# Attention over 32 images: where broadcasts, loads, statistics, one fold and one final step stand in a hand-written order of visits

## Chip, cores and metric

The kernel runs on one core of a Trainium2 chip. The metric is the time of one execution on the device, in microseconds (us); lower is better. Engines are called by the profile's names: PE is TensorE (PEld its weight loads), DVE is VectorE, ACT is ScalarE, POOL is GpSimd, SP is SyncE. In this kernel SP only issues DMAs, and POOL issues some too.

## What is computed

x has 32 images of 256 channels and 32 x 32 pixels. Each image is normalised in 32 groups of 8 channels, goes through causal attention with 8 heads of 32 channels over its 1024 pixels, and the result is added to x. All numbers are float32. Cut to what matters:

```python
def reference(x, q_w, q_b, kv_w, kv_b):
    n = group_norm(x, 32).reshape(B, C, S)            # (g - mean) / sqrt(var + 1e-5)
    q = einsum('oc,bcs->bos', q_w, n) + q_b[None, :, None]
    kv = einsum('oc,bcs->bos', kv_w, n) + kv_b[None, :, None]
    k, v = kv[:, :256], kv[:, 256:]
    q, k, v = to_multihead(q), to_multihead(k), to_multihead(v)
    scores = einsum('bhqd,bhkd->bhqk', q, k) / sqrt(32)
    scores = where(mask == 0, -10000.0, scores)       # a pixel sees earlier pixels alone
    attn = where(mask == 0, 0.0, softmax(scores))
    out = einsum('bhqk,bhkd->bhqd', attn, v)
    return x + out.transpose(0, 1, 3, 2).reshape(B, 256, 32, 32)
```

## The kernel before

The work of one image, called a batch here, is cut into 12 visits (`N = 12`): two groups `g` of four heads, six visits each. A visit takes a set of blocks of keys and queries. Its `scores` (L339) are PE products of `k` and `q` into three PSUM tiles `sT` (L302), three exponentials on ACT into `e` and `eh` (L384, L380), and in visits 0, 1, 3 and 5 of a group a mask on POOL, which writes the tile `diagonal` (L330). One visit later `values` (L399) multiplies the exponentials by `v` on PE into `acc` (L409), and `add_keys` (L421) adds exponentials on DVE, in place (L427). So an addition that overwrites a tile waits until PE has read it.

The softmax is divided out at the end. For each batch there are four sums `n` (two groups of heads by two halves of the queries). Each is 128 partitions by 2048 numbers and is reduced in steps:

- `fold(b, n, 64)` and `fold(b, n, 32)` (L436): DMAs issued by POOL that add the upper half of the partitions to the lower, 512 KB and 256 KB by the profile. The second waits for the first.
- `stack(b, n)` (L442): an SP DMA that puts the remaining 32 partitions into `folded`. It waits for the second fold.
- `sum_folded` (L448): DVE transposes and reductions, in visits 6 and 7 of the next batch.
- `invert` (L485), in visit 8: DVE takes reciprocals, and SP writes them to DRAM (L494) and reads them back four times, broadcast over 32 partitions each, into `rb` (L499). `rb` has one buffer.
- `finish(b, n)` (L519): on DVE a product `num * rb` (L524), two additions of the bias and x (L526) and for the first half a copy of one column (L531), then an SP DMA to the output (L532).

Beside this, a later batch is prepared: four loads of x by SP (L107), two `norm_channels` on DVE (L172: two `BATCH_NORM_STATS2` and an aggregate for 128 channels), `norm_mean` on PE and ACT (`pm`), `norm_deviation` on DVE (`dev`, L195 to L197), `norm_variance` on PE and ACT (`pv`), `norm_rstd` on POOL (L217, L219), `norm_apply` on ACT. The twelve projections of a batch (`pp` and `ppv`, L162) stand one to a visit.

The order is written by hand. Before the program is emitted, each step is entered under the number of a visit with `when`, counted over all batches (batch b begins at visit 12 b). In the main loop a visit i emits its scores, then the steps in `at`, then values and additions of visit i - 1, then the steps in `after`. This order is kept for PE, ACT, DVE and POOL (`manual_schedule`). SP isn't in that list: a scheduler orders its DMAs, and the visit is not a wait. The tables are these, where the numbers in PROJECT and PREPARE count from the first visit of the batch that is prepared:

```python
PREPARE = (-14, -13, -9, -9, -8, -8, -7, -6, -5, -3)
SUMS = (3, 7, 11, 13)
FINISH = (N + 13, N + 13, N + 14, N + 15)
```

The first two of PREPARE are the two `norm_channels`, the third `norm_mean`, the fourth `norm_deviation`, the fifth `norm_variance`. Sum n is folded at SUMS[n] (64 partitions) and two visits later (32), and stacked two visits after that. In visits of a batch, counted modulo 12, the statistics stand in visits 10 and 11, `dev` in 3, the final steps in 1, 1, 2 and 3.

Of the kernel before, what the change touches and what calls it, by code (L numbers as in the profile page):

```python
# [9 lines left out]
F32 = mybir.dt.float32  # L10
# [7 lines left out]
P = 128  # L18
HD = 32
CPG = 8  # L20
HALF = 512
# [11 lines left out]
def tile_norm_attention_residual(  # L33
# [19 lines left out]
    nc = tc.nc  # L53
# [4 lines left out]
    NH = S // HALF  # L58
# [22 lines left out]
        out=avg, in_=avg, pattern=[[-CPG, P // CPG], [0, CPG]],  # L81
# [3 lines left out]
        out=avg, in_=avg, pattern=[[CPG, P // CPG], [0, CPG]],  # L85
# [13 lines left out]
    def unshifted():  # L99
        live = {}  # L100
# [3 lines left out]
        def load_part(b, g, cols):  # L104
            if (g, cols.start) == (0, 0):
                live["x", b] = xpool.tile([P, NG, S], F32, tag="x", name=f"x_{b}")
            nc.sync.dma_start(out=live["x", b][:, g, cols], in_=x_in[b, :, g, cols])  # L107
# [6 lines left out]
        work = tc.alloc_tile_pool(name="work", bufs=2)  # L114
# [3 lines left out]
        dram = tc.alloc_tile_pool(name="dram", bufs=2, space=bass.MemoryType.DRAM)  # L118
# [9 lines left out]
        def load_weights():  # L128
            for n, w in enumerate((q_w, kv_w[0:C], kv_w[C : 2 * C])):
                live["wn", n] = epool.tile([P, 4, HALFBANK], F32, tag="eh", bufs=3, name=f"wn_{n}")[:, :NG, :C]  # L130
                nc.sync.dma_start(out=live["wn", n], in_=w.rearrange("(o p) c -> p o c", p=P))
            nc.sync.dma_start(out=qk_bias[:, 0, :], in_=q_b.rearrange("(g p) -> p g", p=P))
            nc.sync.dma_start(out=qk_bias[:, 1, :], in_=kv_b[0:C].rearrange("(g p) -> p g", p=P))
            nc.sync.dma_start(out=v_bias_col, in_=kv_b[C : 2 * C].rearrange("(g p) -> p g", p=P))
# [346 lines left out]
        def check(rows, least, most):  # L481
            nc.vector.scalar_tensor_tensor(in_range, rows, least, in_range, ALU.is_ge, ALU.mult)
            nc.vector.scalar_tensor_tensor(in_range, rows, most, in_range, ALU.is_le, ALU.mult)

        def invert(b):  # L485
            rows = live["rows", b]
            check(rows, SUM_MIN, SUM_MAX)
            inv = small.tile([P, ROW], F32, tag="inv", name=f"inv_{b}")
            nc.vector.reciprocal(inv, rows)
            turned = small.tile([P, ROW], F32, tag="inv_turned", name=f"inv_turned_{b}")  # L490
            nc.vector.transpose(turned, inv)

            spread = dram.tile([2, 4, 2, HALF], F32, tag="inv", name=f"inverses_{b}")
            nc.sync.dma_start(  # L494
                out=spread.rearrange("a n j (m c) -> (n j m) a c", c=HD), in_=turned.rearrange("p (a c) -> p a c", a=2),
            )
            live["rb", b] = work.tile([P, 4, HALF], F32, tag="rb", bufs=1, name=f"rb_{b}")
            for h in range(4):
                nc.sync.dma_start(  # L499
                    out=live["rb", b][h * HD : (h + 1) * HD],  # L500
                    in_=spread[h // 2, :, h % 2, :].unsqueeze(0).broadcast_to([HD, 4, HALF]),
                )

        def invert_here(b, n, within=slice(0, HALF)):

# [57 lines left out]
        N, TOTAL = NG * len(VISITS), 2  # L563
# [42 lines left out]
        def when(i, f, where=at):  # L606
            where.setdefault(i, []).append(f)
# [11 lines left out]


        PROJECT = (-5, -4, -3, -2, -1, 0, 1, 2, 3, 4, 5, 6)
        PREPARE = (-14, -13, -9, -9, -8, -8, -7, -6, -5, -3)
        SUMS = (3, 7, 11, 13)
        FINISH = (N + 13, N + 13, N + 14, N + 15)
        every = range(4)

        with tc.manual_schedule(engines={ENG.PE, ENG.Activation, ENG.DVE, ENG.Pool}):


            load_weights()  # L630
            if B > 1:
                load(1)
            junk = small.tile([P, 1], F32, tag="most", name="junk")
            nc.scalar.activation(junk, ones, AF.Exp)
            keep_busy(16)
            for g in range(NG):
                norm_channels(0, g)
            norm_mean(0)

            live["less_mean"] = work.tile([P, 4, HALF], F32, tag="folded", bufs=1, name="less_mean")[:, 0, :]  # L640
            for s in range(2):
                nc.scalar.activation(
                    blocks(live["less_mean"], s), blocks(live["x", 0][:, 1, :HALF], s, s == 1), AF.Identity,
                    bias=live["minus_mean", 0][:, 1:2],
                )
            turn_weights(0)
            norm_deviation(0)
            norm_variance(0)
            norm_rstd(0)
            for hf in range(NH):  # L650
                for g in range(NG):
                    norm_apply(0, hf, g)
                if hf == 0:
                    for n in (1, 2):
                        turn_weights(n)
                    keep_busy(3)
                    nc.vector.tensor_scalar_mul(qk_bias[:, 0, :], qk_bias[:, 0, :], SCALE)  # L657
            units = projections(0)
            for n, f in zip((None, None, None, 0, 0, 0) + PROJECT[6:], units):
                if n is None:  # L660
                    f()
                else:
                    when(n, f)
            if B > 1:
                prepare(1, (None, None, 0, 1, 2, 2, 3, 4, 5, 7))
            for b in range(B):
                first, last = b * N, b == B - 1
                if b >= 1:
                    for n, f in zip(PROJECT if not last else PROJECT[:-1] + (7,), projections(b)):
                        when(first + n, f)  # L670
                if b >= 2:
                    for n in range(NG * NH):
                        cols = slice(n % NH * HALF, (n % NH + 1) * HALF)
                        when(max(first - 2 * N + 7 + n // 3, 0), lambda b=b, n=n, cols=cols: load_part(b, n // NH, cols))
                    prepare(b, [first + n for n in PREPARE])
                if not last:
                    for n in every:
                        v = first + SUMS[n]
                        when(v, lambda b=b, n=n: fold(b, n, 2 * HD), after)
                        when(v + 2, lambda b=b, n=n: fold(b, n, HD), after)  # L680
                        when(v + 4, lambda b=b, n=n: stack(b, n))
                    late = b == B - 2
                    v = first + N + (5 if late else 6)
                    when(v, lambda b=b: sum_folded(b, every[:2]), after)
                    when(v + 1, lambda b=b: sum_folded(b, every[2:]), after)
                    when(v + 2, lambda b=b: invert(b))
                    for n in every:
                        v = first + (N + 9 + n // 2 if late else FINISH[n])
                        when(v, lambda b=b, n=n: finish(b, n), after)
                else:  # L690
                    when(first + 3, lambda: sums(0, SUMMED[1], False), after)
                    when(first + 7, lambda: sums(1, SUMMED[5], False), after)
                    when(first + 9, lambda: sums(2, SUMMED[7], False), after)
                    when(first + 8, lambda b=b: invert_here(b, 0))
                    when(first + 9, lambda b=b: finish(b, 0))
                    when(first + 8, lambda b=b: invert_here(b, 1))
                    when(first + 8, lambda b=b: finish(b, 1))
                    when(first + 10, lambda b=b: invert_here(b, 2))
                    when(first + 11, lambda b=b: finish(b, 2), after)
            for i in range(B * N + 1):  # L700
                if i < B * N:
                    scores(*divmod(i, N))
                for f in at.pop(i, ()):
                    f()
                b, v = divmod(i - 1, N)
                if i == B * N:

                    sums(3, SUMMED[v], False)
                if i:
                    values(b, v)  # L710
                    if b < B - 1 or v not in SUMMED or v == 1:
                        add_keys(b, v)
                if i in (B * N - 2, B * N - 1):

                    sums(3, SUMMED[v])
                for f in after.pop(i, ()):
                    f()
            assert not at and not after
            outside = end_last(B - 1)
# [170 lines left out]
```

## Time and profile before

| | |
|---|---|
| median of three runs | 1830.64 us (1828.4 to 1831.34) |
| the profiled execution, its own time | 1833.26 us |
| its span, first to last instruction | 1831.6 us |
| granted TensorE clock, mean | 0.997 of full |
| one batch in the second half (start of a `pv` to that of the next) | 55.77 us |
| DMA traffic | 236.77 MB, mean 129 GB/s |
| POOL's DMA queue, share of 16 engines | 36.4% |
| SP's DMA queue, share of 16 engines | 27.5% |

The profile is of one execution. A line of waits reads "engine tile line <- releaser: total us, times, longest us"; "issue" is time in which the engine waited for nothing that the profile shows. A line of a timeline reads "start us, length us, engine, line, operation, output<-inputs, shapes, count", and in brackets the idle time ahead of it and what ended it; merged lines give the whole stretch. "SPq" and "POOL ... DMA_DIRECT2D" are DMA issues and not the transfers. In the list of DMA queues, the columns are packets, MB and the share of 16 engines' span; q0 is POOL's queue, q1 SP's, q8 and q14 carry instructions.

### The profile page before, as it was taken

The numbers are of one execution on the slowest core, as the hardware profiler recorded it, in microseconds if no ns is written. First come the engines' busy times: TensorE is split into PE (matmuls) and PEld (weight loads), VectorE is DVE, ScalarE is ACT, GpSimd is POOL, SyncE is SP. The second block draws the span as 40 slices with busy tenths as digits, with TensorE's granted clock in tenths as the row PEclk, the third lists the DMA queues.
The fourth block names the chain that finished last, engine by engine and source line by source line (L and its number), as shares of the span: only waits on it lengthen the run. The fifth ranks groups of instructions, "written<-read, shape, count | busy, mean of one in ns | idle before, by whom it ended". The sixth has DMA issues, their size and how long they took to land.

```text
span 1831.6 us, 81672 instructions
## 1 busy us (share of the span) xinstructions
PE 1801.3 (98%) x37036; PEld 961.8 (53%) x37036; DVE 1639.0 (89%) x1832; ACT 1456.0 (79%) x1985; POOL 877.6 (48%) x901
## 2 busy tenths in 40 slices
PE   9999999999999999999999999999999999999997
PEld 5555555555555555555555555555555555555553
DVE  4689999888898988999999999999999998999987
ACT  6888878877788877888877888878888778888784
POOL 2444544534445445454554454554545544545531
PEclk9999999999999999999999999999999999999999
DMA  3457676666755767667767667676676666676662
GB/s 122 66 101 147 129 146 118 122 144 129 148 113 121 152 123 147 117 125 149 142 133 132 123 139 147 136 142 119 122 151 136 137 132 121 139 147 135 123 115 82
DMA packets 86530, 236.77 MB, mean 129 GB/s; under 512 B 21280, under 2 KB 22304, under 8 KB 70304
## 3 DMA queue, kind: packets, MB, share of 16 engines
q0 software_dynamic: 15872, 97.53, 36.4%
q1 hardware_dynamic: 70304, 133.96, 27.5%
q8 instruction: 290, 4.75, 1.0%
q14 instruction: 64, 0.52, 0.1%
HBM read 66.85 MB, written 34.57 MB: 55 GB/s over the span
## 4 chain that ended last, share of the span: by engine, by line
PE 88%; DVE 9%; issue 2%; ACT 0%; DMA 0%; POOL 0%; DVEq 0%
PE sT L302 27%; PE pp L162 26%; PE acc L409 24%; PE ppv L162 10%; DVE diagonal L427 3%; DVE e L427 2%; DVE rb L526 2%; DVE num L524 1%; PE pd L461 0%; PE pv L162 0%; ACT e L384 0%; DMA x<-in_x_dram 0%; DVE dev L197 0%; DVE dev L196 0%; DVE rb L531 0%
## 5 line engine op out<-in xcount | busy, mean ns | idle before, releaser
L384 ACT ACTIVATE e<-sT 128x1024 f32<-128x1024 f32 x768 | 745.0, 1022 | 261.0 <-PE sT L302 261.0
L330 POOL TENSOR_SCALAR_AFFINE_SELECT diagonal<-eh 128x512 f32<-128x512 f32 x512 | 580.8, 1157 | 768.2 <-ACT eh L380 765.7
L302 PE MATMUL sT<-q,k 32*64 32x128 f32 (+2 forms) x18432 | 584.3, 372 | 0.4 <-issue 0.3
L427 DVE TENSOR_TENSOR e<-e,e 128x1024 f32<-128x1024 f32 x315 | 539.3, 1712 | 30.8 <-ACT v L266 13.6
L302 PEld LDWEIGHTS sT<-q,k 32*64 32x64 f32 x18432 | 405.5, 131 | 181.2 <-PE sT L302 59.5
L162 PE MATMUL pp<-xn,wT 128*32 128x512 f32 x4096 | 492.2, 598 | 0.2 <-DVE qk_bias L657 0.2
L409 PE MATMUL acc<-e,v 128*32 128x384 f32 (+3 forms) x4608 | 405.2, 451 | 2.3 <-issue 2.2
L380 ACT ACTIVATE eh<-sT 128x768 f32<-128x768 f32 (+1 forms) x384 | 341.1, 888 | 0.0
L409 PEld LDWEIGHTS acc<-e,v 128*32 128x32 f32 x4608 | 150.9, 110 | 265.1 <-issue 242.4
L162 PE MATMUL ppv<-wT,xn 128*32 128x256 f32 x4096 | 252.8, 383 | 8.4 <-issue 8.4
L162 PEld LDWEIGHTS pp<-xn,wT 128*32 128x32 f32 x4096 | 107.2, 109 | 198.9 <-issue 164.3
L427 DVE TENSOR_TENSOR diagonal<-diagonal,e 128x1536 f32<-128x1536 f32 x126 | 187.9, 1492 | 25.8 <-PE acc L409 10.6
L427 DVE TENSOR_TENSOR e<-e,eh 128x1024 f32<-128x1024 f32 x127 | 179.2, 1411 | 6.5
L409 PEld LDWEIGHTS acc<-diagonal,v 128*32 128x32 f32 x4096 | 124.6, 110 | 86.1 <-issue 73.1
L162 PEld LDWEIGHTS ppv<-wT,xn 128*32 128x32 f32 x4096 | 120.8, 109 | 92.0 <-issue 20.6
L409 PE MATMUL acc<-diagonal,v 128*32 128x128 f32 x4096 | 162.0, 273 | 0.0
L427 DVE TENSOR_TENSOR e<-e,diagonal 128x2048 f32<-128x2048 f32 x62 | 140.5, 2266 | 23.5 <-POOL diagonal L330 23.5
L440 POOL DMA_DIRECT2D e<-e x124 | 111.5, 899 | 75.5 <-issue 38.2
L526 DVE SCALAR_TENSOR_TENSOR rb<-num,v_bias_col,x 128x256 f32<-128x256 f32 x248 | 133.5, 579 | 4.4
L235 ACT ACTIVATE xn<-x,shift,rstd 128x256 f32<-128x256 f32 x248 | 137.1, 613 | 0.0
L427 DVE TENSOR_TENSOR e<-e 128x512 f32<-128x512 f32 x64 | 62.6, 978 | 72.6 <-PE acc L409 72.6
L440 POOL DMA_DIRECT2D diagonal<-diagonal x124 | 111.6, 900 | 0.2 <-issue 0.2
(78 smaller groups left out, 1075.2 us busy)
## 6 DMA issues: line engine op xcount, KB each, us to landing
diagonal<-diagonal POOLq DMA_DIRECT2D x62, 512.0 KB, 6.5
e<-e POOLq DMA_DIRECT2D x62, 512.0 KB, 7.3
rb<-inverses SPq DMA_DIRECT2D x124, 256.0 KB, 4.7
out_dram<-rb SPq DMA_DIRECT2D x124, 256.0 KB, 7.6
x<-in_x_dram SPq DMA_DIRECT2D x120, 256.0 KB, 6.1
diagonal<-diagonal POOLq DMA_DIRECT2D x62, 256.0 KB, 4.6
folded<-diagonal SPq DMA_DIRECT2D x62, 256.0 KB, 6.0
e<-e POOLq DMA_DIRECT2D x62, 256.0 KB, 5.2
```

Source lines behind the costliest of these rows:

```text
L162: nc.tensor.matmul(out[part], lhsT=lhsT[:, part], rhs=rhs, start=start, stop=stop, skip_group_check=True)
L235: nc.scalar.activation(to, of, AF.Identity, bias=live["shift", b][:, g : g + 1], scale=rstd)
L302: return nc.tensor.matmul(bank[c : c + KEYS, cols], lhsT=live["k", b, g][rows, kb * P + c : kb * P + c + KEYS], rhs=live["q", b, g][rows, ...
L330: nc.gpsimd.affine_select(out=square[:, :, place + s * P : place + (s + 1) * P], in_=raw[:, :, (1 - s) * KEYS : (3 - s) * KEYS], pattern=[ ...
L380: exp = nc.scalar.activation(eh.rearrange("p (n bank) q -> p bank n q", n=2)[:, :, :, :narrow], short[:, :, :, :narrow], AF.Exp)
L384: nc.scalar.activation(e[:, 2 * a : 2 * a + 2, :wide], pairs[a][:, :, :wide], AF.Exp)
L409: nc.tensor.matmul(acc[HD * j : HD * (j + 1), of], lhsT=live["v", b][:, kb, h * HD : (h + 1) * HD], rhs=e[:, j, :], start=first, stop=last ...
L427: nc.vector.tensor_add(to, to, tile_of(b, g, at))
L440: nc.gpsimd.dma_start(out=total[:rows], in_=total[rows : 2 * rows], accum_op=ALU.add)
L524: nc.vector.tensor_mul(num, num, rb)
L526: nc.vector.scalar_tensor_tensor(blocks(rb, s), blocks(num, s, s == 1), v_bias_col[:, g : g + 1], blocks(xt[:, g, cols], s), ALU.add, ALU.add,
```

## The change

Nothing is computed differently, and the number of instructions of each kind that work on data is the same. Five things move:

- The write of the inverses stays in `invert`; the four broadcasts become `spread_inverses(b, h)` and are entered under visits 8, 9, 10 and 11 (for the batch before the last all under the same visit as `invert`).
- The four loads of x are entered under visits 7, 8, 11 and 12, where it was 7, 7, 7 and 8.
- The two `norm_channels` are entered two visits later, at -12 and -11.
- The folds and the stack of the third sum are entered one visit earlier, at 10, 12 and 14.
- The last of the four final steps is entered one visit later, at N + 16.

```diff
-            spread = dram.tile([2, 4, 2, HALF], F32, tag="inv", name=f"inverses_{b}")
+            spread = live["spread", b] = dram.tile([2, 4, 2, HALF], F32, tag="inv", name=f"inverses_{b}")
             nc.sync.dma_start(
                 out=spread.rearrange("a n j (m c) -> (n j m) a c", c=HD), in_=turned.rearrange("p (a c) -> p a c", a=2),
             )
-            live["rb", b] = work.tile([P, 4, HALF], F32, tag="rb", bufs=1, name=f"rb_{b}")
-            for h in range(4):
-                nc.sync.dma_start(
-                    out=live["rb", b][h * HD : (h + 1) * HD],
-                    in_=spread[h // 2, :, h % 2, :].unsqueeze(0).broadcast_to([HD, 4, HALF]),
-                )
+
+        def spread_inverses(b, h):
+            if h == 0:
+                live["rb", b] = work.tile([P, 4, HALF], F32, tag="rb", bufs=1, name=f"rb_{b}")
+            nc.sync.dma_start(
+                out=live["rb", b][h * HD : (h + 1) * HD],
+                in_=live["spread", b][h // 2, :, h % 2, :].unsqueeze(0).broadcast_to([HD, 4, HALF]),
+            )
...
-        PREPARE = (-14, -13, -9, -9, -8, -8, -7, -6, -5, -3)
-        SUMS = (3, 7, 11, 13)
-        FINISH = (N + 13, N + 13, N + 14, N + 15)
+        PREPARE = (-12, -11, -9, -9, -8, -8, -7, -6, -5, -3)
+        SUMS = (3, 7, 10, 13)
+        LOADS = (7, 8, 11, 12)
+        FINISH = (N + 13, N + 13, N + 14, N + 16)
...
-                        when(max(first - 2 * N + 7 + n // 3, 0), lambda b=b, n=n, cols=cols: load_part(b, n // NH, cols))
+                        when(max(first - 2 * N + LOADS[n], 0), lambda b=b, n=n, cols=cols: load_part(b, n // NH, cols))
...
                     when(v + 2, lambda b=b: invert(b))
+                    for n in every:
+                        when(v + 2 + (0 if late else n), lambda b=b, n=n: spread_inverses(b, n))
```

## The prediction

> **What bounds the kernel now.** I read the page first, then TensorE's waits in two windows, the chain of waits over one period, and the timelines of VectorE, GpSimd's queue and SP's queue over the same period. The page says that TensorE is busy nearly all the time, so only what still makes it wait can be won:
>
> ```profile
> PE 1801.3 (98%) x37036; PEld 961.8 (53%) x37036; DVE 1639.0 (89%) x1832; ACT 1456.0 (79%) x1985; POOL 877.6 (48%) x901
> q8 instruction: 290, 4.75, 1.0%
> ```
>
> TensorE's waits from 100 to 700 us, then from 700 to 1740 us (columns: total us, times, longest):
>
> ```profile
> PE ppv L162 <- issue: 8.4, 9, 1.9
> PE acc L409 <- issue: 2.2, 2, 1.9
> ```
>
> ```profile
> PE pv L162 <- DVE dev L197: 5.9, 18, 0.3
> ```
>
> Two different losses. In the second half every batch loses 0.33 us, because `pv` (the variance product) waits for `dev`, the end of a VectorE chain. There a batch takes 55.77 us, of which TensorE is busy 55.44. In the first half that wait is absent, and TensorE stops instead with nothing that the profile names, 10.6 us in all, nearly always inside the `ppv` of visit 3.
>
> The chain of waits around one such `pv` (start, us, what) shows how the first loss arises: `dev` stands last in a VectorE queue that has no gap, behind the last of the four final steps.
>
> ```profile
> 776.74 0.61 DVE num L524
> 777.38 0.88 DVE rb L526 x2
> 778.26 0.08 DVE dev L195
> 778.56 0.17 DVE dev L197
> 778.87 0.24 PE pv L162 x5
> ```
>
> The unnamed stops are late instruction fetches. The 290 packets of the instruction queue are TensorE's: 290 x 256 instructions are its 74,000 matmuls and weight loads, so there is a fetch every 256 instructions, nine per batch. In the trace's packets a fetch normally starts when some 160 instructions of the block before it have run. Before the stop at 604.82 us it started only at 602.93, 222 instructions later than that; the GpSimd folds had kept the 16 DMA engines busy since 595.7, and it started when they ended. There are 61 such long bursts (a 256 KB and a 512 KB fold issued together, 7 us). A fetch wanted 1.8 to 2.1 us after a burst's start was served 4.1 to 6 us after it (one at 8.6); one wanted 1 to 1.7 us ahead of it, at +2.3 to +4.7 (one at 6.5); one wanted 2.15 us or more after it, mostly only at its end, 6 to 8.7 us. TensorE stops when the fetch has ended about 415 to 448 instructions into the old block. The boundary moves by two instructions a batch, which is why this ends midway.
>
> GpSimd's folds, with issue time, over one period; the pairs at 877 and 887 are the long bursts, 860.50 and 868.53 are single:
>
> ```profile
> 860.50 0.81 POOL L440 DMA_DIRECT2D e<-e  x1 [1.25 <-issue]
> 868.53 0.84 POOL L440 DMA_DIRECT2D diagonal<-diagonal  x1
> 877.18 0.80 POOL L440 DMA_DIRECT2D diagonal<-diagonal  x1
> 877.71 1.13 POOL L440 DMA_DIRECT2D e<-e  x1
> ```
>
> **What the Trainium skill says.** "Runtime: NRT & Kernel Launch", section "Instruction fetch mechanics": instructions come in 16 KiB blocks of 256 and the cost of a boundary is mostly hidden. The trace agrees on the size (4.75 MB in 290 packets), and not on the cost here, 10.6 us. "DMA: Bandwidth & Descriptors", section "Queues, rings and completion order": each DMA engine takes its queues in turn, a packet at a time. That would let a fetch through soon; the trace shows it held for 5 us, so I use the measured delays. "SBUF — State Buffer", section "SBUF: two separate sides": a VectorE operation with two SBUF inputs and a GpSimd one exclude each other. The trace agrees: the `num` product beside a mask takes 1.11 us, alone 0.68.
>
> **Part by part.**
>
> *Broadcasts and loads, one to a visit.* SP's order isn't written by hand. In the order of the built programs the four `rb` broadcasts still follow the write of the inverses back to back, and the four loads of x still stand together ahead of the stack of the first sum. An SP DMA waits for data, not for a visit: before, they went out as soon as they could,
>
> ```profile
> 837.62 4.45 SPq L107 DMA_DIRECT2D x<-in_x_dram  x4
> 856.33 1.97 SPq L499 DMA_DIRECT2D rb<-inverses  x4
> ```
>
> and will again. Cost and gain 0 (bounds: -1 to +1 us, from the 1.97 us in which they are issued). Cover if the broadcasts did spread: they land about 861.5, `finish` first reads `rb` at 876.7, 15 us of slack.
>
> *Statistics from visits 10 and 11 to 0 and 1.*
>
> ```profile
> 862.64 1.28 DVE L177 BATCH_NORM_STATS2 st<-x 128x6 f32<-128x512 f32 x2
> 863.96 0.21 DVE L178 BATCH_NORM_AGGREGATE mv<-st 128x2 f32<-128x12 f32 x1
> 875.70 1.03 DVE L427 TENSOR_TENSOR e<-e 128x512 f32<-128x512 f32 x1 [1.38 <-PE acc L409]
> 880.54 3.09 DVE L427 TENSOR_TENSOR diagonal<-diagonal,e 128x1536 f32<-128x1536 f32 x2 [0.27 <-issue]
> 889.72 0.15 DVE L195 TENSOR_TENSOR dev<-mv,mean 128x2 f32<-128x2 f32 x1
> ```
>
> Each set is 1.44 us (862.64 to 864.08). Taking both from ahead lets VectorE reach the add at 875.70 earlier, but that add waits for TensorE. The first set fits in the 1.38 us idle there plus the 2.88 us freed, less some 2 us now spent waiting for a mask: free. The second lands between the second final step and the `diagonal` adds: +1.44, of which the 0.27 us wait is swallowed: +1.17 us ahead of `dev`. Its result is needed by `pm` at 885.2 and ready at 881.7. The x that they read was loaded 30 us before.
>
> *The last final step a visit later.* Its product and two additions, 888.21 to 889.72, leave the place ahead of `dev`: -1.51 us. Together 1.17 - 1.51 = -0.34, so `dev` ends at 890.27 - 0.34 = 889.93. `pv` could start at 890.08, 0.14 us after `dev`, so 889.94 is just in time. Overlaps with the mask at 884.27 shift from the additions to a product; I take that as even, +-0.4 us. VectorE has 58 more semaphore instructions, two a batch; those in the trace run under the preceding operation. I leave 0.05 us a batch over 29 batches, 1.5 us: **5.9 - 1.5 = -4.4 us**. Bounds: -5.9, and +9 if `dev` is 0.3 later instead. Its output DMA goes out 4 us later on SP; behind it stand the loads of x, about 1 us later, needed 30 us on. In SP's order the third stack now stands ahead of the first three outputs, which wait about 3 us for its fold; `rb` is rewritten only 30 us later.
>
> *The fold of the third sum, a visit earlier.* Its two DMAs move on GpSimd's queue: the 512 KB one from 868.53 to just behind the 256 KB `e` fold at 860.50, ahead of a mask that starts at 866.32 anyway; the 256 KB one to before a mask, at about 874.9. The latter breaks up the pair at 877, and its burst (878.6 to 885.6) ends about 3 us sooner. That is the burst in which the fetches of the first half were late: 222 instructions late less 3 us x 41 a us is 100, far from a stop. It also frees the 512 KB `e` fold, for which the pair at 887 waits 1.3 us. **-9.6 of the 10.6 us** (bounds 0 and -10.6). In exchange 860.50 becomes a pair: a burst from 862.0 to about 868.5, with a fetch wanted between -1.5 and +0.8 us of its start. By these measurements it is served at about +4.5 where it was at +1.0 to +2.7: 2 us, some 80 to 90 instructions, on ends of 263 to 359. Most stay under 415; about 9 late batches may stop 0.4 us: **+3.5 us** (bounds 0 and +27).
>
> Sum: 1833.26 (the profiled execution, 1.7 us over its span) - 4.4 - 9.6 + 3.5 = 1822.8. The median of the runs is 2.6 us lower than that execution, so 1820.
>
> **Rivals.** *The spread is nothing and the fetches stay late*, because they hang on the outputs and not on the fold: only 4.4 us remain, 1826. For: outputs fill the engines right after that burst. Against: the fetches start with the fold's end. *No change*: the second statistics and a slowed product keep `dev` late and the new pair costs what the old one gives back: 1830. *Slower*: the new pair at 861 holds its fetch to the burst's end, at +6.5 instead of +4.5. A stop of 1 us in each of 27 batches is +27, against -14 gained: 1844. It decides once the fetch is served more than 5 us after it is wanted. Against it: the pairs whose fetch was wanted before +2.1, of which two in over thirty were served that late.
>
> **Chances.** Forecast 0.5 (1814 to 1827), fetches stay late 0.2 (1824 to 1829), no change 0.15 (1827 to 1834), slower 0.15 (1834 to 1850). About 0.2% (3.7 us) is what a measurement can tell from no change. Faster: 0.5 + 0.15 of the second; same 0.05 + 0.15; slower 0.15. The range 1814 to 1834 leaves the slower case out.
>
> **What would show it.** Right: no `pv` wait on `dev`; unnamed stops of TensorE under 4 us; a batch of 55.4 to 55.5 us; SP's four broadcasts still issued within 2 us; the fold pair at 860 instead of 877. Wrong: TensorE stops near the `acc` or `sT` of visits 10 and 11, or `pv` waits on. A longer batch with TensorE fully busy would refute the whole account.

## The result and the profile after

The changed kernel takes 1813.72 us (median of 4 runs, 1813.51 to 1814.04), the kernel before 1829.97 us on the same chip (4 runs, 1828.4 to 1831.34): a ratio of 0.9912, 95% interval 0.9894 to 0.9929. That is 16.25 us less (0.9%), where the prediction had 10 us less. The profiled execution took 1813.86 us, its span is 1812.2 us.

The same two lines of the page as before the change (busy us, share of the span, instructions; then packets, MB and share of the instruction queue):

```profile
PE 1797.5 (99%) x37036; PEld 956.9 (53%) x37036; DVE 1643.0 (91%) x1832; ACT 1457.2 (80%) x1985; POOL 919.4 (51%) x901
q8 instruction: 290, 4.75, 1.1%
```

TensorE's waits from 100 to 1780 us. In the same stretch of the kernel before they were 8.4 us in `ppv`, 5.9 in `pv`, 2.2 in `acc` and 0.3 in `sT`:

```profile
PE sT L302 <- issue: 0.3, 1, 0.3
PE pp L162 <- issue: 0.3, 1, 0.3
PE pv L162 <- DVE dev L197: 0.2, 1, 0.2
```

The chain of waits around one `pv`, and the windows view of one batch, from a `pv` to the next (after the window: its length, then the busy time of PE, PEld, DVE, ACT and POOL, the clock, the DMA share and GB/s):

```profile
763.00 1.29 PE acc L409 x24
764.30 0.12 PE pv L162 x8
764.41 0.90 PE sT L302 x17
```

```profile
764.17:819.61 55.44, 55.44 (x1159) 29.50 (x1153) 51.63 (x58) 45.44 (x62) 29.80 (x28) 1.00 0.68 136
```

The chain no longer leaves TensorE for VectorE. `pv` follows the last `acc` at once, and a batch takes 55.44 us instead of 55.77. Both of the losses that the prediction named are all but gone from the view of waits. TensorE looks full in the 55.44 of this last line. It isn't, as e10 and e11 show below.

GpSimd's queue shows the moved fold, and SP's queue that the spread did nothing: the 512 KB fold of `diagonal` now stands right behind that of `e` at 790.88, the one at 803.90 is single, and the four broadcasts are issued in one go.

```profile
790.88 0.81 POOL L440 DMA_DIRECT2D e<-e  x1 [1.25 <-PE pp L162]
791.43 1.11 POOL L440 DMA_DIRECT2D diagonal<-diagonal  x1
...
803.90 0.78 POOL L440 DMA_DIRECT2D diagonal<-diagonal  x1
```

```profile
787.69 1.76 SPq L501 DMA_DIRECT2D rb<-inverses  x4
```

### The profile page after: what moved, and what is told of

Same layout as the page of the kernel before. It is cut to its first block, busy times and chain, and to the rows that moved or that the text cites. A ratio compares the mean times of both kernels' runs of the same rounds, so it can differ in the third digit from the quotient of the medians.

```text
span 1812.2 us, 81732 instructions
## 1 busy us (share of the span) xinstructions
PE 1797.5 (99%) x37036; PEld 956.9 (53%) x37036; DVE 1643.0 (91%) x1832; ACT 1457.2 (80%) x1985; POOL 919.4 (51%) x901
## 4 chain that ended last, share of the span: by engine, by line
PE 98%; DVE 1%; ACT 0%; issue 0%; DMA 0%; POOL 0%; DVEq 0%
PE sT L302 30%; PE acc L409 27%; PE pp L162 26%; PE ppv L162 13%; PE pd L461 0%; ACT e L384 0%; PE pv L162 0%; DMA x<-in_x_dram 0%; DVE diagonal L427 0%; DVE st L177 0%; DVE e L427 0%; PE pm L162 0%; POOL diagonal L330 0%; ACT eh L380 0%; DVE rb_last L528 0%
## 5 line engine op out<-in xcount | busy, mean ns | idle before, releaser
L330 POOL TENSOR_SCALAR_AFFINE_SELECT diagonal<-eh 128x512 f32<-128x512 f32 x512 | 649.1, 1291 | 748.6 <-ACT eh L380 748.4
L427 DVE TENSOR_TENSOR e<-e,e 128x1024 f32<-128x1024 f32 x315 | 553.6, 1757 | 21.6 <-ACT v L266 4.8
L162 PE MATMUL ppv<-wT,xn 128*32 128x256 f32 x4096 | 247.5, 382 | 0.0
L409 PEld LDWEIGHTS acc<-diagonal,v 128*32 128x32 f32 x4096 | 119.6, 110 | 92.9 <-issue 75.7
L440 POOL DMA_DIRECT2D e<-e x124 | 102.3, 825 | 38.1 <-PE pp L162 31.1
L528 DVE SCALAR_TENSOR_TENSOR rb<-num,v_bias_col,x 128x256 f32<-128x256 f32 x248 | 117.5, 514 | 4.4
L440 POOL DMA_DIRECT2D diagonal<-diagonal x124 | 119.4, 963 | 0.0
L526 DVE TENSOR_TENSOR num<-num,rb 128x512 f32<-128x512 f32 x124 | 110.8, 894 | 0.0
```

What stands on the lines that cost most here:

```text
L162: nc.tensor.matmul(out[part], lhsT=lhsT[:, part], rhs=rhs, start=start, stop=stop, skip_group_check=True)
L330: nc.gpsimd.affine_select(out=square[:, :, place + s * P : place + (s + 1) * P], in_=raw[:, :, (1 - s) * KEYS : (3 - s) * KEYS], pattern=[ ...
L409: nc.tensor.matmul(acc[HD * j : HD * (j + 1), of], lhsT=live["v", b][:, kb, h * HD : (h + 1) * HD], rhs=e[:, j, :], start=first, stop=last ...
L427: nc.vector.tensor_add(to, to, tile_of(b, g, at))
L440: nc.gpsimd.dma_start(out=total[:rows], in_=total[rows : 2 * rows], accum_op=ALU.add)
L526: nc.vector.tensor_mul(num, num, rb)
```

## Experiments

The theory to be tested was that of the prediction: `pv` waits for `dev` until the last final step moves, and late instruction fetches stop TensorE until the pair of folds at 877 is broken up. The rivals: only one of the two pays, or the gain comes from elsewhere (the broadcasts, the loads, the statistics). Each ratio is to the kernel before on the same chip, whose medians lie between 1829.3 and 1831.4 us from one group of runs to the next.

### Each part alone, put into the kernel before

**e1, the fold alone.**

```diff
-        SUMS = (3, 7, 11, 13)
+        SUMS = (3, 7, 10, 13)
```

Expected: 

> Only the third sum's folds move a visit earlier. Two losses (my theory: late instruction fetches behind the paired folds, and pv waiting for dev): the unnamed stops of TensorE fall from 10.6 us to under 1.5, but pv now waits 0.33 us for dev in all 29 batches, 9.6 us where it was 6.3; together -7, about 1823. Rival, one VectorE chain causes both losses: 1830, as nothing moves on VectorE. Rival, the spread of broadcasts and loads does it: 1830.

Measured: 1831.6 us, ratio 1.001 (1.0002 to 1.0017). By itself the fold's move is worth nothing, slightly less. Its waits:

```profile
PE pv L162 <- DVE dev L197: 9.9, 30, 0.4
PE sT L302 <- issue: 6.5, 15, 0.6
```

The stops in `ppv` are gone as foreseen, but the new pair makes 15 others, in `sT` of visit 10. And `pv` now waits in every batch (29 times from 100 us on), where it waited in 18: a batch that had lost its time in `ppv` had given VectorE the time to finish `dev`.

**e2, the final step alone.**

```diff
-        FINISH = (N + 13, N + 13, N + 14, N + 15)
+        FINISH = (N + 13, N + 13, N + 14, N + 16)
```

Expected: 

> Only the last final step moves a visit later. My theory: dev ends 1.5 us earlier, the pv wait (5.9 us) goes, the unnamed stops in the first half stay near 10.6 us: 1824. Rival, one VectorE chain behind both: 1814. Rival, spread: 1830.

Measured: 1821.56 us, ratio 0.9958 (0.9943 to 0.9973). 8.9 us are gained, though the view of waits had shown only 5.9 on `dev` in all. No wait on `dev` is left between batches; the stops in `ppv` stay (7.8 us in 9).

**e3, the statistics alone.**

```diff
-        PREPARE = (-14, -13, -9, -9, -8, -8, -7, -6, -5, -3)
+        PREPARE = (-12, -11, -9, -9, -8, -8, -7, -6, -5, -3)
```

Expected: 

> Only the statistics move two visits later. My theory: dev ends 1.17 us later, so pv waits about 1.5 us in every batch without an unnamed stop: +1.17 x 18 and up to 1.5 x 11, 1851 to 1867, so slower than before. Rival, the statistics are hidden wherever they stand because VectorE has 3.7 us idle in a batch: 1830.

Measured: 1851.45 us, ratio 1.012 (1.0102 to 1.0138).

```profile
PE pv L162 <- DVE dev L197: 30.2, 26, 1.4
```

Most of these waits are 1.38 us where they had been 0.33: the statistics hold `dev` up by 1.05 us a batch, close to the 1.17 of the prediction. Alone this part is a loss.

**e4, broadcasts and loads alone** (the loads at 7, 8, 9 and 10, since the statistics still need x in visits 10 and 11).

```diff
+        LOADS = (7, 8, 9, 10)
...
+                    for n in every:
+                        when(v + 2 + (0 if late else n), lambda b=b, n=n: spread_inverses(b, n))
```

Expected: 

> Only the broadcasts are entered one to a visit and the loads of x at visits 7, 8, 9, 10 (the last two before the statistics, which stand at 10 and 11 here). My theory: SP's queue holds its DMAs in the same order and they go out as soon as data is there: 1830, the four broadcasts issued within 2 us. Rival, the spread frees the DMA engines for the fetches: unnamed stops under 2 us, 1820 or less.

Measured: 1829.96 us, ratio 1.0001 (0.9987 to 1.0015), and the stops are as before: 7.6 us in `ppv`, 6.0 on `dev`.

### Is it the instruction fetch?

TensorE's first work in the kernel is a loop of products that nothing uses, `keep_busy(16)`. Six more or six fewer of its rounds put 24 instructions more or fewer ahead of everything, and so shift where each block of 256 ends against the folds. Nothing else changes.

**e8, 24 instructions more.**

```diff
-            keep_busy(16)
+            keep_busy(22)
```

Expected: 

> The kernel before with six more filler products (24 instructions) on TensorE at the very start, nothing else. If the unnamed stops are late instruction fetches, each boundary of 256 instructions falls 24 instructions earlier, where it stood 12 batches later: the stops of batches 3 to 11 vanish, under 2 us stay, pv waits for dev in all batches instead: -10.6 + 3.6 + up to 2.1 us of the filler itself, 1823 to 1826. If the stops belong to the early batches for another reason (HBM, start of the run): 1830 to 1832, stops of 10 us in the first 650 us.

Measured: 1826.03 us, ratio 0.9975 (0.9968 to 0.9983).

```profile
PE pv L162 <- DVE dev L197: 9.6, 29, 0.4
```

Every stop in `ppv` is gone, without a fold moved. As in e1, `pv` then waits in all batches, so that only 4.5 us of the gain remain. By the starts of the batches, some 6 us are lost beyond these waits (each priced at 0.46 us, as in e12 below), in other places.

**e9, 24 instructions fewer.**

```diff
-            keep_busy(16)
+            keep_busy(10)
```

Expected: 

> The kernel before with six filler products fewer (24 instructions) at the very start. Late fetches: each boundary falls 24 instructions later, so the stops last 12 batches longer, up to about 1320 us instead of 650, some 18 us of stops in all: 1836 to 1840. Another reason tied to the early batches: 1830, stops as before.

Measured: 1861.01 us (1851.29 to 1869.63), ratio 1.0172 (1.0114 to 1.023), far beyond what was expected.

```profile
PE ppv L162 <- issue: 13.4, 16, 2.4
PE acc L409 <- issue: 8.4, 6, 2.4
PE sT L302 <- issue: 6.2, 4, 3.4
```

So the unnamed stops depend on where the boundaries of blocks fall, and on nothing that the 24 instructions compute. In the traces' packets the late fetches follow: of 290, those that ended 415 or more instructions into the old block are 12 in the kernel before, 6 in e8, 29 in e9 and 1 in the changed kernel. The trace shows nothing but the fetch that goes by these boundaries. The runs also show that the kernel before stood by chance in a bearable place.

### One part taken out of the changed kernel

**e5, without the fold's move.**

```diff
-        SUMS = (3, 7, 10, 13)
+        SUMS = (3, 7, 11, 13)
```

Expected: 

> The changed kernel with the third sum's folds back in visits 11, 13, 15. My theory: no pv wait, unnamed stops come back, near 10 us: 1824. Rival, one VectorE chain causes both losses: 1814, no stops.

Measured: 1826.31 us, ratio 0.9981 (0.9972 to 0.999). The stops in `ppv` are back, 6.4 us in 8. With the other parts in place the fold's move is worth 12.6 us (1826.31 to the 1813.72 of the changed kernel), alone it was worth nothing (e1).

**e6, without the final step's move.**

```diff
-        FINISH = (N + 13, N + 13, N + 14, N + 16)
+        FINISH = (N + 13, N + 13, N + 14, N + 15)
```

Expected: 

> The changed kernel with the last final step back in visit 3 (N + 15). My theory: dev ends 1.5 us later than in the changed kernel, pv waits about 1.4 us in each of 29 batches, no unnamed stops: 1814 + 41 = 1855. Rival, VectorE's idle time takes it up: 1814.

Measured: 1861.87 us, ratio 1.0178 (1.0162 to 1.0195): `pv` waits 37.6 us on `dev` in 30 waits, and 6.4 us of stops stand in `sT`. The time is 7 us over the theory's 1855, which had no such stops.

**e7, without the statistics' move.**

```diff
-        PREPARE = (-12, -11, -9, -9, -8, -8, -7, -6, -5, -3)
-        LOADS = (7, 8, 11, 12)
+        PREPARE = (-14, -13, -9, -9, -8, -8, -7, -6, -5, -3)
+        LOADS = (7, 8, 9, 10)
```

Expected: 

> The changed kernel with the statistics back at visits 10 and 11 (and so the last two loads entered at visits 9 and 10). My theory: dev ends another 1.2 us earlier than needed, nothing won and nothing lost: 1814, no pv wait, no unnamed stops. Rival, moving the statistics is part of the gain (it takes VectorE's load off visits 10 and 11): 1816 or more.

Measured: 1819.1 us (1817.78 to 1822.56), ratio 0.9945 (0.993 to 0.996). This missed: the part that loses 21 us alone gains 5.4 here.

```profile
PE sT L302 <- issue: 5.8, 15, 0.6
```

The new pair stops TensorE in `sT` as in e1, and in the changed kernel it hardly does. What differs is when the pair goes out. In the trace's DMA packets, over 28 batches (times from the batch's `pv`, those of the fetch from the start of the burst; medians):

| | `e` fold issued | burst starts | fetch wanted | served | ended over 400 instructions into the old block |
|---|---|---|---|---|---|
| e7 | 25.85 | 27.3 | +0.55 | +4.1 | 8 of 28 |
| changed kernel | 26.71 | 28.65 | -0.85 | +2.05 | 1 of 28 |

The pair is 0.86 us later in the changed kernel and the burst 1.35, and then most fetches are wanted before the burst begins. Set beside the starts of a batch of e11 (below), which has no stop there, 21 of 29 batches of e7 lose time at this place, 13.0 us in all, where the view of waits shows 5.8 us in `sT` and 1.3 in `pp`. In 12 of the 21 the fetch ended only 334 to 387 instructions into the old block, so the count of those over 400 is too low a measure. In the changed kernel 3 batches lose 1.4 us there.

The mask in front of the pair explains most of the delay, 0.73 of the 0.86 us (GpSimd's queue; first the changed kernel, its `pv` at 764.17, then e7, its `pv` at 766.8):

```profile
786.36 3.27 POOL L330 TENSOR_SCALAR_AFFINE_SELECT diagonal<-eh 128x512 f32<-128x512 f32 x2 [6.50 <-ACT eh L380]
```

```profile
788.82 2.54 POOL L330 TENSOR_SCALAR_AFFINE_SELECT diagonal<-eh 128x512 f32<-128x512 f32 x2 [6.37 <-ACT eh L380]
```

With the statistics moved, VectorE reaches its addition of `diagonal` 0.9 us later in the batch (20.3 and 19.4 us after `pv`), and that addition covers more of the mask. VectorE's lines, again the changed kernel first:

```profile
784.47 3.09 DVE L427 TENSOR_TENSOR diagonal<-diagonal,e 128x1536 f32<-128x1536 f32 x2
```

```profile
786.21 3.09 DVE L427 TENSOR_TENSOR diagonal<-diagonal,e 128x1536 f32<-128x1536 f32 x2
```

"SBUF — State Buffer", section "SBUF: two separate sides", says that a VectorE operation with two SBUF inputs and a GpSimd one that reads SBUF exclude each other; both traces agree, 3.27 against 2.54 us for the same mask. So the statistics would gain by an accident: they delay a mask, which delays a pair. That was then put to the test.

### Is it the delay of the pair?

**e10: e7, with the pair held up by something else.** Six memsets on GpSimd stand in front of it.

```diff
             if (n, rows) == (1, HD):
                 nc.gpsimd.drain()
+                for _ in range(6):
+                    nc.gpsimd.memset(inv_last, 1.0)
```

Expected: 

> The changed kernel with the statistics left in visits 10 and 11, as in e7, and six small memsets on GpSimd (about 0.14 us each, a constant tile that is rewritten with other contents, read by nothing until the end) between the mask of visit 9 and the pair of folds, so that the pair goes out about 0.85 us later, where the statistics' move had put it. Theory: the move of the statistics gains only because VectorE then holds up that mask and with it the pair, so the fetch gets ahead of the burst; with the memsets the stops in sT of visit 10 (5.8 us in 15 stops in e7) fall under 1 us, and the time goes from 1819.1 to 1814-1815.5. Rival: the statistics' own place matters (VectorE's queue ahead of a wait of TensorE), and the memsets change nothing or cost: 1818-1821, stops as in e7.

Measured: 1809.52 us (1808.15 to 1811.85), ratio 0.9888 (0.987 to 0.9905). The `e` fold goes out 26.70 us after `pv`, as in the changed kernel. The burst starts at 28.1, the fetch is wanted 0.2 us ahead of it and served at +2.7 (medians), and 2 of 28 end over 400 instructions into the old block. In `sT` two stops are left:

```profile
PE sT L302 <- issue: 1.5, 2, 1.3
```

So the delay of the pair by itself is worth some 9.6 us (1819.1 to 1809.52, on two chips on which the kernel before took 1829.26 and 1829.65), more than the whole gain of the statistics' move, 5.4. That the memsets do better than the statistics, by 4.2 us, the expectation had not foreseen. Start to start, a batch takes 55.31 us here in most cases, against 55.45 in the changed kernel. The order of TensorE's instructions is the same in both, so I compared their starts within a batch: the step of 0.14 us comes at the `acc` of a `diagonal`, 13.5 us after `pv`. The mask for it, in the changed kernel and then in e7:

```profile
772.83 4.73 POOL L330 TENSOR_SCALAR_AFFINE_SELECT diagonal<-eh 128x512 f32<-128x512 f32 x2 [1.09 <-ACT eh L380]
```

```profile
775.43 3.72 POOL L330 TENSOR_SCALAR_AFFINE_SELECT diagonal<-eh 128x512 f32<-128x512 f32 x2 [2.11 <-ACT eh L380]
```

VectorE's lateness stretches this mask too, by 1.0 us, and its last piece, a memset (L337), now ends too late. Who waits for that memset, in the changed kernel:

```profile
  PEld acc L409: 5.6, 28
```

In e7, e10 and the kernel before, nobody waits for it. In e5, where the statistics and the final step are moved too, the weight loads wait for it 18 times, and a batch mostly takes 55.43 us there. The wait stands in the view of the weight loads, not in that of the products. No run takes this wait away by itself, so its price is read from the starts, 0.14 us a batch.

**e11: no pair at all.** e7 again, but the third sum's first fold stays in visit 11, and only its second fold and its stack come a visit earlier.

```diff
-        SUMS = (3, 7, 10, 13)
+        SUMS = (3, 7, 11, 13)
...
-                        when(v + 2, lambda b=b, n=n: fold(b, n, HD), after)
-                        when(v + 4, lambda b=b, n=n: stack(b, n))
+                        when(v + (1 if n == 2 else 2), lambda b=b, n=n: fold(b, n, HD), after)
+                        when(v + (3 if n == 2 else 4), lambda b=b, n=n: stack(b, n))
```

Expected: 

> As e7 (the changed kernel with the statistics left in visits 10 and 11), but the third sum's first fold stays in visit 11, as before the change, and only its second fold and its stack come a visit earlier. So neither the pair at 860 nor the one at 877 is formed. Theory: with no long burst near a boundary that is wanted, neither ppv of visit 3 nor sT of visit 10 stops, and pv doesn't wait, since the finish is moved: 1814-1816, unnamed stops under 2 us. Rival: a fold in another place holds the fetch as well, or GpSimd's queue is held by the second fold and delays masks: 1818-1826.

Measured: 1806.02 us (1805.76 to 1807.87), ratio 0.9871 (0.9854 to 0.9888), below what either theory had said. TensorE's waits from 100 to 1780 us:

```profile
PE sT L302 <- issue: 0.5, 1, 0.5
```

Of the 29 batches 27 take 55.31 us. It beats both kernels, the changed one by 7.7 us (0.4%).

### What does the wait for `dev` cost?

e11 opened a question on the first term of the prediction: if a batch takes 55.31 us without waits, then the 55.44 that the prediction took as TensorE's work contains some.

**e12: e11 with the final step in its old place.**

```diff
-        FINISH = (N + 13, N + 13, N + 14, N + 16)
+        FINISH = (N + 13, N + 13, N + 14, N + 15)
```

Expected: 

> As e11 (no pair at 860, none at 877, statistics in visits 10 and 11), but the last final step is back in its place of before, so that pv waits for dev in every batch and nothing else stops TensorE. This measures the price of the dev wait by itself over 29 batches. Theory: the batch without any wait is 55.31 us (as in e11), and the gap that the trace shows as 0.33 us costs 0.46, since the modelled ends of the matmuls ahead of it hide 0.13: 1806.0 + 29 x 0.46 = 1819.4, batches of 55.77. Rival, the prediction's reading: the batch without the wait is 55.44 and the wait costs the 0.33 that the view of waits shows: 1806.0 + 29 x 0.33 = 1815.6, batches of 55.64.

Measured: 1819.5 us (1819.18 to 1820.3), ratio 0.994 (0.9925 to 0.9954). The theory's number, to 0.1 us. TensorE's waits from 100 to 1780 us:

```profile
PE pv L162 <- DVE dev L197: 9.7, 29, 0.3
```

TensorE's timeline at one `pv`, and the windows view of the batch after it, first e11:

```profile
816.22 0.62 PE L409 MATMUL acc<-diagonal,v 128*32 128x128 f32 x16
816.70 0.24 PE L162 MATMUL pv<-dev,avg 128*32 128x2 f32 x8
```

```profile
816.70:872.01 55.31, 55.31 (x1160) 29.55 (x1152) 52.23 (x58) 45.38 (x62) 26.01 (x28) 1.00 0.69 136
```

Then e12:

```profile
822.22 0.62 PE L409 MATMUL acc<-diagonal,v 128*32 128x128 f32 x16
823.17 0.24 PE L162 MATMUL pv<-dev,avg 128*32 128x2 f32 x8 [0.33 <-DVE dev L197]
```

```profile
823.17:878.95 55.78, 55.45 (x1153) 29.58 (x1153) 52.17 (x58) 45.37 (x62) 28.86 (x28) 1.00 0.69 135
```

Without the wait `pv` starts 0.48 us after the group of `acc`, ahead of the 0.62 at which that group ends by the profile. With it, it starts 0.95 after. The wait costs the difference of the starts, 0.47 us, and the profile shows 0.33, for it counts from the modelled end. The missing 0.14 is booked as busy time: 55.45 against 55.31 for the same work.

## Why the prediction was too high

The mechanisms of the prediction held, and every sign that it gave for being right came: no wait of `pv` on `dev` but one of 0.2 us, unnamed stops of 0.6 us, a batch of 55.44 us, the broadcasts in one go, the pair at 860. Its sizes did not hold. The runs can be chained, so that each step differs in one thing, apart from the spread of broadcasts and loads, worth nothing by e4, and the memsets of e10 (medians in us):

| from, to | what differs | predicted | measured |
|---|---|---|---|
| before to e12: 1831.4 to 1819.5 | the pair at 877 is broken up | -9.6 | -11.9 |
| e12 to e11: 1819.5 to 1806.0 | the last final step a visit later | -5.9 + 1.5 | -13.5 |
| e11 to e10: 1806.0 to 1809.5 | the new pair, at its later time | +3.5 | +3.5 |
| e10 to the changed kernel: 1809.5 to 1813.7 | the statistics, all but the delay of the pair | 0 | +4.2 |

The predicted column sums to -10.5. The measured one sums to -17.7 from the 1831.4 of that group's runs of before. The -16.25 of the result starts from 1829.97. The first and the last step are the least certain: by the interval of e12's ratio the -11.9 lies between -8 and -14, and the last step goes from one group of runs to another.

**What failed is the size of both losses**, "5.9 - 1.5 = -4.4 us" and "-9.6 of the 10.6 us". Both were read as the idle time that the view of waits shows, with "TensorE is busy 55.44" as the floor. The floor is 55.31 (e11), and counted from start to start both losses are larger:

- A wait on `dev` costs 0.46 or 0.47 us and not 0.33 (e12). With the stops still there, the 18 waits of the trace are then 8.3 us and not 5.9, and 8.9 were measured (e2).
- In the profile of the kernel before, the 11 batches without such a wait take 17.4 us more than 11 x 55.31, where the view shows stops of 10.6.

The two losses also overlap. The prediction saw that "in the first half that wait is absent" but not why: the stops in `ppv`, just ahead of `pv`, gave `dev` its time. Take the stops away (e1, e8, e12) and `pv` waits in nearly every batch, 28 or 29 of 29. So how the gain is shared out depends on the order. In the table the pair goes first: of the 17.4 us, 11 x 0.46 = 5.1 come back as waits, which leaves 12.3, and 11.9 were measured. Then the final step ends 29 waits: 29 x 0.46 is 13.3, and 13.5 were measured. With the final step first it is 8.9 (e2), then 15.5 (e2 to e11). Both together are 23.6 us (e11), where 5.9 and 9.6 had been put.

**The 1.5 us for more semaphore instructions and a close `dev`** is not seen at `pv`: only one wait of 0.2 us on `dev` is left between 100 and 1780 us.

**The statistics** do cost ahead of `dev` what the prediction said, 1.05 us against 1.17 (e3), and the final step pays for it. What it left out is that VectorE then stays late, by 1 us eight us after `pv` and by 0.9 us twenty us after it. This has two effects beyond `dev`, both through the mask on GpSimd: +4.2 us by the mask at 772.83, whose memset TensorE's weight loads await (29 x 0.14 is 4.1), and, by the measure of e10, -9.6 us by the mask at 786.36, which delays the new pair.

**The late fetches** were the right cause (e8, e9), and breaking up the pair at 877 cured them. "Runtime: NRT & Kernel Launch", section "Instruction fetch mechanics", calls the cost of a boundary mostly hidden. Here breaking up one pair was worth 11.9 us, and e9 lost 30 us more than the kernel before by a shift of the boundaries.

**The new pair's +3.5** agrees by luck. Where the prediction put the pair (860.50, 25.86 us after its `pv` at 834.64, the place that it has in e7), it costs 13.1 us (e11 to e7), though the fetch is served at +4.1 there, close to the forecast +4.5. The step that failed is "Most stay under 415": that limit had been read at `ppv`, and in `sT` of e7 TensorE lost time with ends from 334 instructions on (some up to 356 lost none), in 21 batches where 9 were forecast. e1 fits this: -11.9 for the old pair and +13.1 for the new one make +1.2, and 1.2 were measured. In the changed kernel the pair goes out 0.86 us later, and the price falls to about 3.5. The "slower" rival named this mechanism. But its sign, a fetch served more than 5 us after it is wanted, isn't what decided: in e7 it is 3.6 us.

**The spread of broadcasts and loads** was rightly put at 0 (e4).

What stays open: in the profile of e10 four batches take more than 55.31 us, by 0.8, 1.1, 3.4 and 0.5, in that of e11 two, by 1.4 and 0.15. The difference, 4.3 us, covers the 3.5 between the two kernels. The first two are late fetches at the new pair; why the longest, at 1150 us, is long in both is open. Why the fetch gets ahead of a burst that starts later follows from the times at which it is wanted; in which order the DMA engines serve the two was not measured. And no run shifts the boundaries of blocks in the changed kernel or in e11, so how far the prices of the new pair hang on where the boundaries happen to lie is not known.

## What to carry to other kernels

Price a wait or a stop by the starts of the instructions around it, with and without the wait, and not by the idle time that a modelled end leaves: here 5.9 us shown were 8.3, and 10.6 shown were 17.4. When two stalls follow each other on the bounding engine, the first hides the second. The first cured alone then gives less than it costs, so count the second in every period from which the first goes. And before a long burst of transfers is moved, look at when the bounding engine next needs instructions.

## What was unexpected of the hardware

- 24 instructions more or fewer among the unused products at the start of the kernel took its time from 1830.5 us to 1826.0 (e8) or to 1861.0 (e9).
- Moving a pair of fold DMAs by 0.86 us, with nothing else changed but six memsets, was worth 9.6 us (e7 to e10).
- The view of waits showed about half of what late fetches cost TensorE: 10.6 us where the batches were 17.4 us longer (the kernel before), 7.1 where 13.0 were lost (e7).
- Two masks on GpSimd took 3.72 us or 4.73 us, and others 2.54 or 3.27, according to how much of VectorE's additions lay beside them.
- A stop of 0.14 us in each batch showed in no idle time of TensorE's products. It was in the view of the weight loads, as 0.2 us each.
